# A graph attention kernel: the softmax's denominators are summed over partitions by VectorE instead of TensorE

## The chip, the core and the metric

The kernel runs on one core of a Trainium2 chip. A core has TensorE (PE: matrix products, and transposes by a product with the identity), VectorE (DVE), ScalarE (ACT), GpSimd (POOL) and SyncE (SP, which here only starts DMAs). Each works through a queue of its own in order, and semaphores tie the queues together. The metric is the device time of one execution in microseconds (us). SBUF is the on-chip memory of 128 partitions, PSUM the memory that TensorE writes; a quadrant is a group of 32 partitions.

## What is computed

x is 3327 x 512, adj is 3327 x 3327 with ones in about 1% of its places and zeros elsewhere. Two graph attention layers are followed by a layer norm, a binarized linear layer with an aggregation over adj, and another layer norm.

```python
def _gat_layer(x, W, adj):
    proj = x @ W
    Wh, Ws = jnp.split(proj, 2, axis=-1)
    scores = Wh @ Ws.T
    a = jax.nn.softmax(scores, axis=-1) * adj
    out = a @ Wh
    out = out + x
    return jax.nn.leaky_relu(out, NEG_SLOPE)
...
x = _layernorm(x + _L0_gnn_ref(x, adj, L0_gnn_W_stack), axis=-1)
x = _layernorm(x + _L1_gnn_ref(x, adj, L1_gnn_weight), axis=-1)
```

The softmax runs over all 3327 nodes before adj masks it. So each output row needs a denominator: the sum of its 3327 exponentials, masked or not. The kernel divides by it at the end, on the finished row of a @ Wh.

## The kernel before, in words

The nodes are cut into 26 tiles of 128 rows. Two tiles make a pair of 256, so there are NQ = 13 pairs. For each of the two attention layers, project() prepares the operands, and attention() goes through 13 x 13 steps (g, q): g is the pair of output rows, q the pair of nodes that is summed over. Scores are held transposed: the 256 output rows of g lie along the free axis, the nodes of q on the partitions. All products of 256 x 256 blocks are done as seven products instead of eight, so that sums of blocks are formed on VectorE and GpSimd, and results are put together from PSUM on VectorE and ScalarE.

A step of the loop at L976 writes out by hand, in the order of a number between 0 and 1 that each piece of work carries, what the queues get. For attention step v that is:

- TensorE: the score products of a later pair (L582, banks Z, X, Y in PSUM), and for step v itself the seven products with the values (L808).
- ScalarE: copies of the score products out of PSUM (L599, L634, L639), and the exponential of step v + 3 (L730). TensorE's next product into a bank waits for the copy out of it.
- VectorE: sums that put the scores together (L609, L624, L630), the running maximum (L652), the subtraction of the column maximum for step v + 3 (L727), the running sum of exponentials for step v + 2 (L738), the mask by adj (L743), and in half of the steps block sums of adj and a check of it (L763, L772).
- GpSimd: four block sums of the masked scores (L781 to L784), which wait for L743, and which TensorE's L808 needs.
- SyncE: the loads.

The running sum (L738) leaves for each g a tile total[g] of 128 partitions x 2 x 256: on each partition, the exponentials of its share of the nodes, for the 256 output rows of g. When the last step of g is done, take_out() (L818) puts the rows together from PSUM (L831 to L842), and finish(g) (L844) hands back a list of functions, one of which is called in each following step at 0.7 (L1005). GpSimd first adds the two halves of total[g] (L847). The first of the functions is norm():

```python
for i in range(2):
    nc.tensor.transpose(pz[:, i], sm[:, ts(i, P)], ident)
nc.vector.reduce_sum(rz, pz, axis=AX.X)
nc.vector.reciprocal(rz, rz)
```

Two transposes on TensorE (L856) bring the 256 rows onto the partitions of a PSUM tile pz, VectorE sums each over the free axis (L857) and takes the reciprocal (L858). The functions behind it, residual(i), scale the rows by rz (L872), apply the leaky relu (L875), add x in the last layer (L879), and store through GpSimd's DMA queue. In the last layer sign(i), turn(i) and linear(i) follow: layer norm statistics and signs on VectorE (L887, L888, L890), transposes of the signs (L896, copied by L898) and the binary product (L906).

There are 13 such normalizations in each of the two layers, 26 in all. The last one of layer 0 (g = 12) stands between attention and the next layer's project(): behind it on VectorE are the two residuals and then block sums of the new operands (L206 to L210), which TensorE's L403 needs. In the last layer VectorE also forms sums for the final aggregation during the last pair g = 12 (product_sums, L1076: L213 to L216), and the normalization of g = 12 stands at the end of attention, where TensorE is filled with aggregation products (L1100).

Of the kernel before, what the change touches and what calls it, by code (L numbers as in the profile page):

```python
# [9 lines left out]
F32 = mybir.dt.float32  # L10
# [6 lines left out]
AX = mybir.AxisListType  # L17
PSUM = bass.MemoryType.PSUM

P = 128  # L20
CT = 4
CW = CT * P
B = 32
HW = CW // 2
# [6 lines left out]
def kernel(  # L31
# [8 lines left out]
    nc = tc.nc  # L40
# [9 lines left out]
    def rows(t):  # L50
        return min(P, N - t * P)
# [7 lines left out]
    def half_tiles(g):  # L59

        return (2 * g, 2 * g + 1)
# [8 lines left out]
    small = ctx.enter_context(tc.tile_pool(name="small", bufs=4))  # L70
    ps_ch = ctx.enter_context(tc.tile_pool(name="ps_ch", bufs=3, space=PSUM))
    ps_acc = ctx.enter_context(tc.tile_pool(name="ps_acc", bufs=4, space=PSUM))
    ps_tr = ctx.enter_context(tc.tile_pool(name="ps_tr", bufs=1, space=PSUM))
# [7 lines left out]
    ident = keep.tile([P, P], F32, name="ident")  # L81
# [30 lines left out]
    def load_rows(eng, dst, src, r):  # L112

        cut = r - r % 16
        engines = eng if isinstance(eng, tuple) else (eng,)
        if cut:
            engines[0].dma_start(out=dst[:cut], in_=src[:cut])
        if cut < r:
            engines[-1].dma_start(out=dst[cut:r], in_=src[cut:r])
# [431 lines left out]
    def attention(l, att):  # L551
# [5 lines left out]
        sc, top, total, off, adj, acc, gs, xs, ch = ({} for _ in range(9))  # L557
# [286 lines left out]
        def finish(g):  # L844

            sm = total[g][:, 0]
            nc.gpsimd.tensor_tensor(sm, sm, total[g][:, 1], ALU.add)  # L847
            pz = ps_tr.tile([P, 2, P], F32, tag="tr", name=f"pz_{l}_{g}")
            rz = small.tile([P, 2], F32, tag="rz", name=f"rz_{l}_{g}")
            hs = out_.pop(g)  # L850
            mine = half_tiles(g)
            held = {}

            def norm():
                for i in range(2):
                    nc.tensor.transpose(pz[:, i], sm[:, ts(i, P)], ident)  # L856
                nc.vector.reduce_sum(rz, pz, axis=AX.X)  # L857
                nc.vector.reciprocal(rz, rz)  # L858

            def fetch(i):  # L860
                t = mine[i]
                span = slice(t * P, t * P + rows(t))
                for name, src in (("xres", x1_d), ("x0", x)) if last else (("xres", x),):
                    xr = ring.tile([P, D], F32, tag="xr", name=f"{name}_{l}_{t}")
                    load_rows(nc.sync, xr, src[span, :], rows(t))
                    held[i, name] = xr

            def residual(i):
                t, hh = mine[i], hs[i]
                r = rows(t)  # L870
                span = slice(t * P, t * P + r)
                nc.vector.scalar_tensor_tensor(  # L872
                    hh[:r], hh[:r], rz[:r, i : i + 1], held[i, "xres"][:r], ALU.mult, ALU.add
                )
                nc.vector.scalar_tensor_tensor(  # L875
                    hh[:r], hh[:r], NEG_SLOPE, hh[:r], ALU.mult, ALU.max
                )
                if last:
                    nc.vector.tensor_tensor(hh[:r], hh[:r], held[i, "x0"][:r], ALU.add)  # L879
                load_rows(nc.gpsimd, h_d[span, :] if last else x1_d[span, :], hh, r)  # L880

            def sign(i):

                t, hh = mine[i], hs[i]
                r = rows(t)
                st = small.tile([P, 6], F32, tag="bn", name=f"bn_{t}")
                nc.vector.bn_stats(st[:r], hh[:r])  # L887
                nc.vector.bn_aggr(mv[:r, t, :], st[:r])  # L888
                ba = held[i] = att.tile([P, D], BF16, tag="ba", bufs=1, name=f"ba_{t}")
                nc.vector.tensor_scalar(ba[:r], hh[:r], mv[:r, t, 0:1], None, ALU.is_gt)  # L890

            def turn(i):
                r = rows(mine[i])
                pt = ps_tr.tile([P, KD, P], BF16, tag="tr", name=f"pbt_{mine[i]}")
                for k in range(KD):
                    nc.tensor.transpose(pt[:, k, :r], held[i][:r, ts(k, P)], ident_h[:r, :r])  # L896
                held[i] = att.tile([P, KD, P], BF16, tag="baT", bufs=1, name=f"baT_{mine[i]}")
                nc.scalar.copy(held[i][:, :, :r], pt[:, :, :r])  # L898

            def linear(i):  # L900

                t = mine[i]
                r = rows(t)
                pw = ps_tr.tile([P, D], F32, tag="tr", name=f"pxw_{t}")
                for k in range(KD):
                    nc.tensor.matmul(  # L906
                        pw[:r], held[i][:, k, :r], bw[k], start=(k == 0), stop=(k == KD - 1)
                    )
                if g >= NQ - 2:
                    nc.scalar.copy(xw[t][:r], pw[:r])  # L910
                    return
                xh = att.tile([P, D], F16, tag="ba", bufs=1, name=f"xwh_{t}")
                nc.scalar.copy(xh[:r], pw[:r])
                load_rows(nc.gpsimd, xw_d[t], xh, r)

            fetch(0)
            if not last:
                return [norm, lambda: residual(0), lambda: fetch(1), lambda: None,
                        lambda: residual(1)]
            free = [] if g == NQ - 1 else [lambda: None]  # L920
            return [
                norm, lambda: residual(0), lambda: (sign(0), fetch(1)), *free,
                lambda: turn(0), lambda: linear(0), lambda: residual(1), lambda: sign(1), *free,
                lambda: turn(1), lambda: linear(1),
            ]
# [50 lines left out]
        for v in range(-LOOK - 4, len(steps)):  # L976
            u = v + LOOK
# [33 lines left out]
            if last and 0 <= v - first_products < EARLY:  # L1011
                p = v - first_products
# [3 lines left out]
            if v >= 0 and steps[v][1] == NQ - 1:  # L1016
                later += finish(steps[v][0])
# [309 lines left out]
```

## Time and profile before

| what | before |
|---|---|
| time, median of 3 runs | 2633.66 us (2631.25 to 2634.98) |
| the profiled execution | 2629.29 us, its span 2627.5 us |
| VectorE busy | 2089.6 us, 4279 instructions |
| TensorE busy | 2594.9 us, 12656 matmuls |
| ScalarE, GpSimd busy | 788.1 us, 1098.4 us |
| L856, transposes into pz | 52, median 273 ns |
| L857, the sum from PSUM | 26, median 412 ns |
| L858, the reciprocal | 26, median 165 ns |
| L847, GpSimd's sum of halves | 26, median 737 ns |

The profile is one execution. Its page gives the busy time of each engine, the same in 40 slices of the span (each digit is tenths of a slice), the chain of work that ended last, and groups of instructions: line, engine, operation, output<-input, shapes, count | busy time, mean ns of one | idle time of the engine just before, and what ended it. A list of waits names who waited for whom: us in total, times, longest. A timeline line has the start, the time taken, engine, line, operation, and in brackets the idle time before it and what ended that. Matmuls are pipelined and each lasts longer than it holds its engine, so the distance between starts tells what one costs; on VectorE, too, an instruction may start a little ahead of the end of the one before.

### The profile page before, as it was taken

Reading aid. Unit: us, or ns where it says so; the run is one execution under the profiler, and the core shown is the slowest. Engines: PE = TensorE matmul, PEld = TensorE weight load, DVE = VectorE, ACT = ScalarE, POOL = GpSimd, SP = SyncE. Lnnn points to the kernel's source line nnn. Section 1 sums busy time; section 2 is a strip of 40 time slices with the busy share of each in tenths; the row PEclk is TensorE's granted clock in tenths of the full one; section 3 lists DMA queues with packets and bytes.
Section 4 is the critical chain, followed back from the end, with each engine's and each line's share of the span. In section 5 each row is a group of like instructions: output and inputs, shape, how many; then the busy total and the mean of one; then the engine's idle time right before and its main releaser. Section 6 shows DMA issues by size and latency. Waiting matters only on the chain. (4 is left out here: it accounts for less than half of the span.)

```text
span 2627.5 us, 40294 instructions
## 1 busy us (share of the span) xinstructions
PE 2594.9 (99%) x12656; PEld 2249.1 (86%) x12656; DVE 2089.6 (80%) x4279; ACT 788.1 (30%) x1954; POOL 1098.4 (42%) x2025
## 2 busy tenths in 40 slices
PE   9999999999999999999999999999999999999998
PEld 6888888888888888887888888888888888888787
DVE  5864888889898886677875689888898888767976
ACT  2323332333333332222232333333333333222143
POOL 2640344444444444546552134444444444455510
PEclk9999999999999999999999999999999999999999
DMA  6855777787777776797865678777777777677775
GB/s 202 297 196 177 241 239 266 239 275 253 264 243 244 263 245 222 237 256 243 295 235 182 226 229 277 248 236 266 240 275 249 236 267 238 223 262 257 265 246 176
DMA packets 308055, 639.17 MB, mean 243 GB/s; under 512 B 34855, under 2 KB 175745, under 8 KB 306298
## 3 DMA queue, kind: packets, MB, share of 16 engines
q1 hardware_dynamic: 272140, 530.29, 61.9%
q0 software_dynamic: 35664, 106.18, 11.0%
q8 instruction: 104, 1.70, 0.3%
q14 instruction: 117, 0.96, 0.1%
q10 hardware_dynamic: 30, 0.03, 0.0%
HBM read 529.69 MB, written 106.67 MB: 242 GB/s over the span
## 5 line engine op out<-in xcount | busy, mean ns | idle before, releaser
L582 PE MATMUL pZ<-gs,xs 128*128 128x256 f32 x2496 | 636.0, 379 | 1.3 <-ACT u L599 1.3
L781 POOL TENSOR_TENSOR as<-s 128x128 f32<-128x128 f32 x338 | 162.4, 480 | 1048.1 <-DVE s L743 720.1
L582 PEld LDWEIGHTS pZ<-gs,xs 128*128 128x128 f32 x2496 | 473.5, 190 | 66.7 <-ACT u L599 2.4
L808 PE MATMUL acc<-ws,s 128*128 128x256 f32 x1352 | 402.2, 379 | 0.0
L808 PE MATMUL acc<-wh,s 128*128 128x256 f32 x1352 | 355.7, 379 | 0.6 <-DVE s L743 0.4
L808 PE MATMUL acc<-ws,as 128*128 128x256 f32 x1352 | 349.8, 380 | 3.9 <-POOL as L783 3.6
L730 ACT ACTIVATE s<-s 128x512 f32<-128x512 f32 x338 | 213.4, 631 | 362.8 <-DVE s L727 362.5
L582 PE MATMUL pY<-gs,xs 128*128 128x256 f32 x1248 | 320.8, 379 | 1.4 <-ACT p L599 1.4
L808 PEld LDWEIGHTS acc<-ws,as 128*128 128x128 f32 x1352 | 255.1, 190 | 44.6 <-POOL as L783 5.7
L808 PEld LDWEIGHTS acc<-wh,s 128*128 128x128 f32 x1352 | 256.6, 190 | 36.3 <-DVE s L743 1.5
L808 PEld LDWEIGHTS acc<-ws,s 128*128 128x128 f32 x1352 | 255.1, 190 | 33.9
L652 DVE TENSOR_TENSOR top<-top,s 128x512 f32<-128x512 f32 x312 | 223.7, 730 | 71.6 <-ACT s L639 51.8
L582 PEld LDWEIGHTS pY<-gs,xs 128*128 128x128 f32 x1248 | 236.6, 190 | 35.4 <-ACT p L599 3.3
L727 DVE TENSOR_TENSOR s<-s,off 128x512 f32<-128x512 f32 x338 | 247.1, 731 | 0.1
L743 DVE TENSOR_TENSOR s<-s,adj 128x512 f32<-128x512 f32 x338 | 237.5, 703 | 9.5 <-DMA adj<-in_adjT_dram 0.7
L738 DVE TENSOR_TENSOR total<-total,s 128x512 f32<-128x512 f32 x312 | 232.3, 745 | 0.0
L599 ACT COPY u<-pZ 128x256 f32<-128x256 f32 x312 | 115.8, 371 | 347.2 <-PE pZ L582 345.6
L783 POOL TENSOR_TENSOR as<-s 128x128 f32<-128x128 f32 x338 | 207.5, 614 | 26.5
L808 PE MATMUL acc<-wh,as 128*128 128x256 f32 x676 | 202.5, 381 | 0.0
L782 POOL TENSOR_TENSOR s<-s 128x128 f32<-128x128 f32 x338 | 184.9, 547 | 27.4
L784 POOL TENSOR_TENSOR as<-s,as 128x128 f32<-128x128 f32 x338 | 181.0, 535 | 26.5
L624 DVE TENSOR_TENSOR s<-p,u 128x256 f32<-128x256 f32 x156 | 66.7, 428 | 145.8 <-ACT u L599 144.8
(220 smaller groups left out, 3866.0 us busy)
## 6 DMA issues: line engine op xcount, KB each, us to landing
ws<-ws_d SPq DMA_DIRECT2D x338, 512.0 KB, 3.8
xs<-xs_d SPq DMA_DIRECT2D x182, 512.0 KB, 5.7
adj<-in_adjT_dram SPq DMA_DIRECT2D x324, 256.0 KB, 4.3
xs<-xs_d SPq DMA_DIRECT2D x156, 384.0 KB, 6.2
gs_d<-gsp POOLq DMA_DIRECT2D x88, 256.0 KB, 2.9
gs<-gs_d SPq DMA_DIRECT2D x12, 1792.0 KB, 10.4
adj_d<-ab POOLq DMA_DIRECT2D x169, 112.0 KB, 4.1
ahl<-adj_d SPq DMA_DIRECT2D x78, 224.0 KB, 4.9
```

The lines of the kernel that those rows point to most:

```text
L582: nc.tensor.matmul(ch[bank], xs[c, q, a][:, k], gs[c][:, b, k], start=(start and k == 0), stop=(k == 1), skip_group_check=True,)
L599: nc.scalar.copy(ch[name], ch[bank])
L652: nc.vector.tensor_tensor(top[i], top[i], t, ALU.max)
L727: nc.vector.tensor_tensor(s, s, off[g].to_broadcast([P, 2, HW]), ALU.subtract)
L730: nc.scalar.activation(sc[g, q], sc[g, q], AF.Exp)
L738: nc.vector.tensor_tensor(total[g], total[g], sc[g, q], ALU.add)
L743: nc.vector.tensor_tensor(s, s, adj[g, q], ALU.mult)
L781: nc.gpsimd.tensor_tensor(s3, a11, a21, ALU.subtract)
L782: nc.gpsimd.tensor_tensor(a21, a21, a22, ALU.add)
L783: nc.gpsimd.tensor_tensor(s2, a21, a11, ALU.subtract)
L784: nc.gpsimd.tensor_tensor(s4, a12, s2, ALU.subtract)
L808: nc.tensor.matmul(acc[g][i // 2][:, i % 2], a[i], b[i], start=(q == 0 and i % 2 == 0), stop=(q == NQ - 1), skip_group_check=True,)
```

## The change

norm() no longer uses TensorE. VectorE transposes the 128 x 256 tile in blocks of 32 x 32 into the second half of total[g], which is no longer needed. In each block the sums over its 32 nodes are then sums along the free axis: one reduce gives 8 numbers on each partition. Each quadrant of partitions then holds the sums over its own 32 of the 128 partitions, so four copies bring the quadrants beside each other on the first one, a second reduce adds the four, and four copies carry the results to the quadrants where the rows of rz lie. The reciprocal stays. The PSUM tile pz is gone; three small SBUF tiles are new.

```diff
-            pz = ps_tr.tile([P, 2, P], F32, tag="tr", name=f"pz_{l}_{g}")
             rz = small.tile([P, 2], F32, tag="rz", name=f"rz_{l}_{g}")
...
             def norm():
-                for i in range(2):
-                    nc.tensor.transpose(pz[:, i], sm[:, ts(i, P)], ident)
-                nc.vector.reduce_sum(rz, pz, axis=AX.X)
+                w = P // B
+                part = small.tile([P, HW // B], F32, tag="zq", bufs=1, name=f"zq_{l}_{g}")
+                quad = small.tile([P, w, HW // B], F32, tag="z4", bufs=1, name=f"z4_{l}_{g}")
+                whole = small.tile([P, 2, w], F32, tag="z", bufs=1, name=f"z_{l}_{g}")
+                turned = total[g][:, 1]
+                nc.vector.transpose(turned, sm)
+                nc.vector.reduce_sum(
+                    part, turned.rearrange("p (r u) -> p r u", u=B), axis=AX.X
+                )
+                for a in range(w):
+                    nc.vector.tensor_copy(quad[:B, a], part[ts(a, B)])
+                nc.vector.reduce_sum(
+                    whole[:B].rearrange("p i r -> p (i r)"),
+                    quad[:B].rearrange("p a r -> p r a"), axis=AX.X,
+                )
+                for a in range(w):
+                    nc.vector.tensor_copy(rz[ts(a, B)], whole[:B, :, a])
                 nc.vector.reciprocal(rz, rz)
```

B is 32, P is 128, HW is 256. ts(a, B) is the a-th group of B partitions.

## The prediction

> **What bounds the kernel now.** I read the page first: busy shares, the slices, the chain that ended last. Then the groups of the lines concerned, TensorE's waits, and the timeline around each of the 26 normalizations.
>
> ```profile
> PE 2594.9 (99%) x12656; PEld 2249.1 (86%) x12656; DVE 2089.6 (80%) x4279; ACT 788.1 (30%) x1954; POOL 1098.4 (42%) x2025
> ...
> PE   9999999999999999999999999999999999999998
> ...
> DVE  5864888889898886677875689888898888767976
> ```
>
> TensorE is busy in 99% of the span, in every slice, at full clock (PEclk is 9 throughout): whatever leaves its queue shortens the kernel, unless another engine is then late. VectorE has 20% idle on average, but 8 and 9 tenths in the attention slices, so its cover has to be looked at place by place. The chain of waits says the same: its largest shares are TensorE's products (L1100, L808), and everything else is 1% or less.
>
> TensorE's waits over the whole span are few; these are the ones that matter here:
>
> ```profile
> PE acc L808 <- POOL as L783: 3.6, 4, 1.2
> PE pZ_wh L403 <- DVE s L207: 2.5, 1, 2.5
> PE agg L1100 <- DVE wh L214: 1.8, 1, 1.8
> ...
> PE pZ L582 <- ACT u L599: 1.3, 2, 0.6
> ```
>
> Behind all four stands VectorE: GpSimd's L783 waits for L743, ScalarE's L599 stands in its queue behind the exponential L730, which waits for L727. So there are already places where VectorE, and not TensorE, sets the pace.
>
> What is removed, from the timeline of TensorE:
>
> ```profile
> 362.45 1.03 PE L582 MATMUL pZ<-gs,xs 128*128 128x256 f32 x4
> 363.32 0.38 PE L856 MATMUL pz<-ident,total 128*128 128x128 f32 x2
> 363.54 0.60 PE L808 MATMUL acc<-wh,as 128*128 128x256 f32 x2
> ```
>
> The starts count, since the durations overlap: the pair of transposes holds the queue from 363.32 to 363.54, 0.22 us.
>
> [...] L99, one element, 153 ns; L857, 256 elements, 415 ns[...]. [...] No row of before moves between quadrants. [...] Here L736, a copy, takes 411 to 683 ns[...].
>
> **The change, part by part.** The instruction order of both programs is the same on all engines but for the lines of norm(): nothing else moves, and no DMA.
>
> Removed from TensorE: 52 transposes, 26 x 0.22 = 5.7 us at most. With them goes the PSUM tile and VectorE's wait for it (4.9 us, six times), all at places with much spare, so it is worth nothing. GpSimd's sum L847 stays, and VectorE now waits for it; the transposes waited for it already and stood ahead of the reduce, so it is over in time in every case, and I cost that wait at nothing.
>
> Added to VectorE, prices from these rows (busy, mean ns):
>
> ```profile
> L340 DVE STREAM_TRANSPOSE xT<-xr 128x512 f32<-128x512 f32 x44 | 47.9, 1096 | 0.0
> ...
> L857 DVE TENSOR_REDUCE rz<-pz 128x2 f32<-128x256 f32 x26 | 10.8, 415 | 4.9 <-PE pz L856 4.9
> ...
> L262 DVE STREAM_TRANSPOSE wTs<-wl 128x128 f32<-128x128 f32 x32 | 7.0, 276 | 0.0
> ...
> L99 DVE TENSOR_SCALAR there<-there 128x1 f32<-128x1 f32 x1 | 0.2, 153 | 0.0
> ```
>
> - Block transpose 128x256: L262 is 0.27 us for 128 elements, 0.13 of it elements; 256 give 0.40. At L340's rate (its reads are strided) it would be 0.55. I take 0.40.
> - Reduce to 8 sums: 0.41, as L857.
> - Reduce of 32 elements: [...]0.19, between L99's 0.15 and L98's 0.28 for 127.
> - Eight tiny copies, in two sets of four. Each is 0.15 (L99). Independent small instructions start early in this trace: after the reciprocal (0.17) the next starts 0.08 later. If the copies do so, a set is 3 x 0.08 + 0.15 = 0.39. But each copy after the first starts in another quadrant; if they are held, a set is 4 x 0.15 = 0.60. I take held, and keep 0.39 as the other end.
> - Five handovers where an instruction waits for its forerunner: 0.035 each (reduce 364.80 + 0.41, reciprocal 365.24), 0.17.
>
> Sum 0.40 + 0.41 + 0.60 + 0.19 + 0.60 + 0.17 = 2.37; minus the old reduce with its handover, 0.45: VectorE's queue grows by d = 1.9 us per normalization (1.5 if nothing is held), 50 us in all. It needs 1.9 us of cover each time. Queued behind it: L652 and L727, hence ScalarE's exponential L730 and the PSUM copies behind that, hence TensorE's next product into those banks; and L743, hence GpSimd's sums and TensorE's L808.
>
> How much cover there is I read from the timeline: from each L858 on, along VectorE's queue and those it releases, counting as spare only what an instruction waited for something else, to the first TensorE instruction that would be late. An example with none (VectorE has no gap from 1832.0 on):
>
> ```profile
> 1840.86 0.68 DVE L727 TENSOR_TENSOR s<-s,off 128x512 f32<-128x512 f32 x1
> ...
> 1841.58 0.63 ACT L730 ACTIVATE s<-s 128x512 f32<-128x512 f32 x1 [4.85 <-DVE s L727]
> ...
> 1842.11 0.35 ACT L599 COPY u<-pZ 128x256 f32<-128x256 f32 x1
> ...
> 1842.52 0.73 PEld L582 LDWEIGHTS pZ<-gs,xs 128*128 128x128 f32 x4 [1.05 <-ACT u L599]
> 1842.52 1.13 PE L582 MATMUL pZ<-gs,xs 128*128 128x256 f32 x4 [0.65 <-ACT u L599]
> ```
>
> TensorE already stands 0.65 us for this chain; anything added to VectorE ahead of it is added to the time. The 26 fall into three groups (start of the reduce, us):
> - Much spare, 2.7 to 6.2 us: 365, 684, 1001, 1074, 1136, 1195, 2238, 2314, 2378. Nothing is lost, the pair is gained: 9 x -0.22 = -2.0.
> - Some, 1.0 to 1.6, in sum 14.4: 526, 607, 845, 926, 1583, 1666, 1749, 1911, 1994, 2077. TensorE is late by 1.9 minus spare: 10 x 1.9 - 14.4 = +4.6.
> - Little, 0 to 0.8, in sum 1.9: 447 (0.45), 766 (0.38), 1243 (0.10, the end of layer 0: L403 waits for L207), 1832 and 2160 (0), 2437 (0.18: TensorE waits for L743 and L783 until 2474), 2486 (0.80: L896 waits for ba, L890). 7 x 1.9 - 1.9 = +11.4.
>
> In the last two groups the removed pair gives nothing, since TensorE would only wait longer. Sum -2.0 + 4.6 + 11.4 = +14.0 us. The profiled execution has a span of 2627.5 and a time of 2629.3, so it would come to 2643.3. It lies 4.4 below the median of the runs, 2633.7; the difference is put on that median: 2647.7.
>
> **The rivals.** (1) The copies overlap, d = 1.5: -2.0, +0.4 (some of the ten still gain), 7 x 1.5 - 1.9 = +8.6: +7.0, 2640.7. For it: the early starts seen above. Against: no such start in the trace crosses quadrants.
> (2) The copies are shut out by GpSimd. In 11 of the 26 places GpSimd's sums run beside where the new instructions will stand; six of these have little or some spare (1243, 1583, 1666, 1911, 1994, 2437), with about two instructions of 0.8 us: up to 6 x 1.6 = 9.6, I take 7: +21, 2654.7. Against: copies of 8 and 2 elements may slip between.
> (3) Not slower: VectorE's readers have the spare after all, since 20% of it is idle. One mechanism, the cover of the 19 places of groups two and three; it decides where d is under about 0.9 us, or the spare is a microsecond more than I read. If only 1243, 2437 and 2486 lose, at d = 1.9 4.6 us, against 23 x 0.22 = 5.1 gained: -0.4, 2633.2. All hidden: -5.7, 2628.0. Against: the waits at 1842.5 and 2170, already open before.
>
> That the change does nothing is excluded: TensorE's order loses exactly the 26 pairs.
>
> **How the numbers follow.** Forecast (held, 1.7 to 2.1 us) 0.57, own range 2643 to 2652; rival 1 0.20; rival 2 0.13; rival 3 0.10. About 0.2% (5.3 us) is what can be told from no change. Rival 1 ends within it in a third of its cases, the forecast hardly; rival 3 lies within it or below: faster 0.04, same 0.14, slower 0.82. The range leaves out most of rival 3 and the far end of rival 2: 2638 to 2656.
>
> **What would show it.** The new copies' rows: mean near 150 ns and starts 0.15 apart (0.08: rival 1; several at 0.5 and more with GpSimd busy: rival 2). Normalization to next instruction 2.4 us on VectorE against 0.52. TensorE's waits: L582 <- ACT L599 from 1.3 us to about 12, L403 <- L207 from 2.5 to above 4, L808 <- L783 up by over 1. VectorE busy up by about 50 us, TensorE down by 52 instructions. If TensorE's waits stay near those of before, the reading of spare was wrong; if they grow although the rows are short, the prices were.

## The result, and the profile after

| | before | after |
|---|---|---|
| median of five runs | 2633.66 us (2629.16 to 2634.98) | 2661.10 us (2659.04 to 2666.74) |
| ratio | | 1.0114, interval 1.0103 to 1.0125 |
| the profiled execution, its span | 2629.29, 2627.5 us | 2666.74, 2664.9 us |

The changed kernel is slower by 27.4 us between the medians, where 14.0 was forecast; 2661.1 lies outside the range. (The two medians alone give a ratio of 1.0104, inside the interval.) The profiled execution of after is the slowest of its five, and its span is 37.4 us above that of before. The traces show where those 37.4 us go; they overstate the 27.4.

From the page of after, the busy shares:

```profile
PE 2602.0 (98%) x12604; PEld 2244.8 (84%) x12604; DVE 2145.1 (80%) x4539; ACT 782.3 (29%) x1954; POOL 1099.7 (41%) x2025
```

TensorE has 52 instructions fewer and VectorE is busy for 55.5 us more, as forecast (52 and about 50). The rows of the new instructions, in the groups by line (busy us, mean ns of one, idle time before):

```profile
L861 DVE STREAM_TRANSPOSE total<-total 128x256 f32<-128x256 f32 x26 | 11.3, 434 | 0.0
L862 DVE TENSOR_REDUCE zq<-total 128x8 f32<-128x256 f32 x26 | 10.9, 420 | 0.9
L866 DVE COPY z<-zq 32x8 f32<-32x8 f32 x104 | 23.0, 221 | 2.0
L867 DVE TENSOR_REDUCE z<-z 32x8 f32<-32x32 f32 x26 | 5.1, 195 | 0.9
L872 DVE COPY rz<-z 32x2 f32<-32x2 f32 x104 | 16.9, 163 | 2.0
```

The prices were nearly right: 0.43 for 0.40, 0.42 for 0.41, 0.195 for 0.19, copies of 0.158 in the middle for 0.15. (For 32 elements a straight line between L99 of before, one element in 153 ns, and L98, 127 in 279 ns, gives an estimate of 184 ns; L867 took 195. The 0.41 came from L857, which reads PSUM and took 415 ns; L862 reads SBUF and took 420.) One normalization on VectorE's timeline, first in before and then in after:

```profile
364.80 0.41 DVE L857 TENSOR_REDUCE rz<-pz 128x2 f32<-128x256 f32 x1
365.24 0.17 DVE L858 RECIPROCAL rz<-rz 128x2 f32<-128x2 f32 x1
365.32 0.67 DVE L652 TENSOR_TENSOR top<-top,s 128x512 f32<-128x512 f32 x1
```

```profile
365.18 0.43 DVE L861 STREAM_TRANSPOSE total<-total 128x256 f32<-128x256 f32 x1
365.64 0.42 DVE L862 TENSOR_REDUCE zq<-total 128x8 f32<-128x256 f32 x1
366.10 0.68 DVE L866 COPY z<-zq 32x8 f32<-32x8 f32 x4
366.81 0.19 DVE L867 TENSOR_REDUCE z<-z 32x8 f32<-32x32 f32 x1
367.04 0.68 DVE L872 COPY rz<-z 32x2 f32<-32x2 f32 x4
367.75 0.17 DVE L873 RECIPROCAL rz<-rz 128x2 f32<-128x2 f32 x1
367.83 0.67 DVE L652 TENSOR_TENSOR top<-top,s 128x512 f32<-128x512 f32 x1
```

A set of four copies takes 0.68 us, not 0.60, and the copies start 0.172 us apart: each starts 13 to 14 ns after the one before has ended. From the transpose to the next instruction, 367.83 - 365.18, are 2.65 us, against 365.32 - 364.80 = 0.52 in before. So VectorE's queue grows by d = 2.13 us, not 1.9, at thirteen of the 26 places, by 2.35 to 2.6 at the twelve where GpSimd's sums run beside it, and by 5.0 at the end of layer 0.

TensorE's waits in after (us in total, times, longest), in the order of the list, and below them one of before:

```profile
PE pZ L582 <- ACT u L599: 13.1, 10, 2.4
PE pY L582 <- ACT p L599: 9.1, 9, 2.3
PE acc L808 <- POOL as L783: 5.6, 6, 1.6
PE pZ_wh L403 <- DVE s L207: 5.0, 1, 5.0
...
PE pD L582 <- DMA xs<-xs_d: 2.4, 3, 1.1
PE pX L582 <- DVE s L630: 2.1, 6, 0.4
PE agg L1115 <- DVE wh L214: 1.8, 1, 1.8
```

```profile
PE pY L582 <- ACT p L599: 1.4, 4, 0.5
```

The first went from 1.3 to 13.1 us (forecast: about 12), the third from 3.6 to 5.6, the fourth from 2.5 to 5.0, all as named. The second, which went from 1.4 us to 9.1, was not named. It leads to a part of the loss that was missed. The place at 1832 in before looks like this in after's timeline:

```profile
1864.69 0.68 DVE L727 TENSOR_TENSOR s<-s,off 128x512 f32<-128x512 f32 x1
...
1865.41 0.63 ACT L730 ACTIVATE s<-s 128x512 f32<-128x512 f32 x1 [6.69 <-DVE s L727]
1865.95 0.36 ACT L599 COPY u<-pZ 128x256 f32<-128x256 f32 x1
...
1866.35 2.07 PE L582 MATMUL pZ<-gs,xs 128*128 128x256 f32 x4 [2.39 <-ACT u L599]
```

The chain is that of the prediction, and the wait that was 0.65 us is 2.39.

**Where the loss lies.** Leaving out the transposes of norm(), the n-th product of TensorE is the same in both traces. The difference between its two start times is its shift, and the growth of the shift shows what TensorE has lost in a stretch, here from 3 us ahead of one normalization (a place) to 3 us ahead of the next:

| group of places | forecast | forecast's rule with the measured d | after less before |
|---|---|---|---|
| much spare, 9 | -2.0 | -2.0 | +1.8 |
| some, 10 | +4.6 | +8.3 | +17.2 |
| little, 7 | +11.4 | +13.6 | +17.9 |
| sum | +14.0 | +19.9 | +36.9 |

The rest of the 37.4 us lies ahead of the first normalization (0.4) and behind TensorE's last product. At 1243, the end of layer 0, d is 5.0 us, so that the rule would put +4.9 there, but TensorE lost only 2.2; the third column has 2.2 there. The residuals behind that normalization took 1.44, 1.66, 1.75 and 0.69 us in before, beside GpSimd's block sums, and 0.75, 0.69, 0.74 and 0.69 in after, where those sums had run beside the new copies instead. The middle group lost twice what even the measured d explains.

**A first reading of the difference.** Adjacency blocks go into a ring, two tiles that are used in turn (tag adj_b), from which a store (L766, adj_d<-ab) takes them away. The store is issued by GpSimd, in its queue behind L784, which needs VectorE's L743. One such store behind the place at 1749, and the next instruction that writes its tile, first in before and then in after:

```profile
1771.66 0.55 POOL L766 DMA_DIRECT2D adj_d<-ab  x1
...
1775.86 0.29 DVE L763 TENSOR_TENSOR ab<-adj 128x128 fp8e4<-128x128 f32 x1 [0.19 <-DMA adj_d<-ab]
```

```profile
1792.21 0.55 POOL L766 DMA_DIRECT2D adj_d<-ab  x1
...
1800.72 0.29 DVE L763 TENSOR_TENSOR ab<-adj 128x128 fp8e4<-128x128 f32 x1 [4.50 <-DMA adj_d<-ab]
1800.77 0.40 ACT L749 CAST ab<-adj 128x256 fp8e4<-128x256 f32 x1 [5.16 <-DMA adj_d<-ab]
...
1801.76 0.37 ACT L599 COPY p<-pY 128x256 f32<-128x256 f32 x1
...
1802.18 0.48 PE L582 MATMUL pY<-gs,xs 128*128 128x256 f32 x1 [2.29 <-ACT p L599]
```

The store issued at 1792.21 frees its tile some 8.5 us later; in before that took 4.2. VectorE and ScalarE, each with an instruction that writes the next block at the head of its queue, stand until then; the PSUM copy L599 stands behind ScalarE's instruction, and TensorE behind that copy. Over the span VectorE's and ScalarE's waits for such stores grew, in before and then in after:

```profile
ACT ab L749 <- DMA adj_d<-ab: 28.1, 17, 4.8
DVE ab L763 <- DMA adj_d<-ab: 22.1, 15, 3.5
```

```profile
DVE ab L763 <- DMA adj_d<-ab: 38.8, 23, 4.5
ACT ab L749 <- DMA adj_d<-ab: 38.5, 17, 5.2
```

Measured against TensorE's own progress, 44 of the 169 stores were issued over 1 us later than in before, by up to 2.4 us. At six of the ten places of the middle group (607, 926, 1583, 1749, 1911, 2077) TensorE was late a second time in this way, 21 to 32 us behind the normalization: 0.7 to 2.6 us each, 8.4 in sum. Without these six losses the group lost 8.8 us, and the rule with the measured d gives 8.3. The six stores were issued 1.4 to 2.0 us later than in before, and they also took 1.0 to 4.3 us longer to land.

### The profile page after: what moved, and what is told of

Read it like the earlier page. It is cut to its first block, busy times and chain, and to the rows that moved or that the text cites. A ratio compares the mean times of both kernels' runs of the same rounds, so it can differ in the third digit from the quotient of the medians.

```text
span 2664.9 us, 40425 instructions
## 1 busy us (share of the span) xinstructions
PE 2602.0 (98%) x12604; PEld 2244.8 (84%) x12604; DVE 2145.1 (80%) x4539; ACT 782.3 (29%) x1954; POOL 1099.7 (41%) x2025
## 5 line engine op out<-in xcount | busy, mean ns | idle before, releaser
L582 PE MATMUL pZ<-gs,xs 128*128 128x256 f32 x2496 | 638.7, 380 | 13.3 <-ACT u L599 13.1
L808 PE MATMUL acc<-ws,s 128*128 128x256 f32 x1352 | 402.2, 379 | 0.0
L808 PE MATMUL acc<-wh,s 128*128 128x256 f32 x1352 | 357.4, 381 | 0.7 <-DVE s L743 0.6
L808 PE MATMUL acc<-ws,as 128*128 128x256 f32 x1352 | 350.1, 380 | 6.0 <-POOL as L783 5.6
L808 PEld LDWEIGHTS acc<-ws,as 128*128 128x128 f32 x1352 | 254.9, 190 | 47.7 <-POOL as L783 8.5
L808 PEld LDWEIGHTS acc<-wh,s 128*128 128x128 f32 x1352 | 257.7, 191 | 37.3 <-DVE s L743 2.1
L808 PEld LDWEIGHTS acc<-ws,s 128*128 128x128 f32 x1352 | 255.1, 190 | 33.9
L582 PEld LDWEIGHTS pY<-gs,xs 128*128 128x128 f32 x1248 | 236.8, 190 | 45.2 <-ACT p L599 13.1
L743 DVE TENSOR_TENSOR s<-s,adj 128x512 f32<-128x512 f32 x338 | 238.4, 705 | 10.2 <-DMA adj<-in_adjT_dram 1.5
L599 ACT COPY u<-pZ 128x256 f32<-128x256 f32 x312 | 115.5, 370 | 304.1 <-PE pZ L582 301.1
L808 PE MATMUL acc<-wh,as 128*128 128x256 f32 x676 | 202.4, 381 | 0.0
L784 POOL TENSOR_TENSOR as<-s,as 128x128 f32<-128x128 f32 x338 | 181.5, 537 | 26.5
```

The costliest lines, as they stand in the source:

```text
L582: nc.tensor.matmul(ch[bank], xs[c, q, a][:, k], gs[c][:, b, k], start=(start and k == 0), stop=(k == 1), skip_group_check=True,)
L599: nc.scalar.copy(ch[name], ch[bank])
L743: nc.vector.tensor_tensor(s, s, adj[g, q], ALU.mult)
L784: nc.gpsimd.tensor_tensor(s4, a12, s2, ALU.subtract)
L808: nc.tensor.matmul(acc[g][i // 2][:, i % 2], a[i], b[i], start=(q == 0 and i % 2 == 0), stop=(q == NQ - 1), skip_group_check=True,)
```

## The experiments

Three theories stood at the start. A is the forecast's own, with the measured d: only what exceeds the spare of a place is added. B says that VectorE's delay is multiplied, by the stores that are issued and land later, and by TensorE's clock after long stalls. C says that reading and transposing the tile costs in itself. Every experiment was run beside the kernel before on the same chip; the medians of before were 2629.8 to 2631.7 us there, and differences are taken from the one beside it. Each diff is against the kernel after or before, as named ahead of it. Where a sum or a copy is left out, the reciprocal is taken of ones, and the softmax is then not normalized.

### Transposes and row sums only

Against after; the second row sum and the last four copies, in the gap, are left out too.

```diff
-                for a in range(w):
-                    nc.vector.tensor_copy(quad[:B, a], part[ts(a, B)])
...
-                nc.vector.reciprocal(rz, rz)
+                nc.vector.reciprocal(rz, ones[:, 0:2])
```

> The changed kernel without its second reduce and its eight copies; the reciprocal is taken of ones, so the rows are not divided by their sums. VectorE's queue then grows by about 0.4 us per normalization (0.47 + 0.42 against 0.53 us to the next instruction). Theory A (time added is what exceeds the spare of each place, nothing else): three places with no spare lose 0.3 each, nearly all others gain the 0.22 of the removed pair: -3 us against before. Theory B (whatever VectorE loses is multiplied, by stores of adj blocks that are issued and land later, and by TensorE's clock): the same sign only if no chain starts, -3 to +2. Rival C (the transpose or reading SBUF instead of PSUM is itself what costs): above +8.

Measured: 2627.14 us, ratio 0.999 (0.9983 to 0.9996), -3.1 us. d is 0.35 us at most places of its trace. C, which expected more than +8, falls: transpose and row sum cost no more than their time on VectorE.

### All copies within one quadrant

Against after:

```diff
-                    nc.vector.tensor_copy(quad[:B, a], part[ts(a, B)])
+                    nc.vector.tensor_copy(quad[:B, a], part[:B])
...
-                    nc.vector.tensor_copy(rz[ts(a, B)], whole[:B, :, a])
-                nc.vector.reciprocal(rz, rz)
+                    nc.vector.tensor_copy(same[:B, a], whole[:B, :, a])
+                nc.vector.reciprocal(rz, ones[:, 0:2])
```

The same eight copies of the same sizes, but none starts in another quadrant than the one before.

> The changed kernel with all eight copies reading and writing in the first quadrant, same count and sizes; the sums are not moved between quadrants and the reciprocal is of ones, so the rows are not divided by their sums. If crossing quadrants is what holds the copies, they start about 0.08 us apart instead of 0.17, and the normalization takes about 2.0 us to the next instruction instead of 2.66: theory A +6 us against before, theory B up to +12. If the copies are spaced by their own length whatever the quadrant, all stays as in the changed kernel: +25 to +29 us.

Measured: 2645.41 us, ratio 1.0054 (1.004 to 1.0067), +15.2 us. From its timeline on VectorE:

```profile
363.85 0.38 DVE L867 COPY z<-zq 32x8 f32<-32x8 f32 x4
364.26 0.20 DVE L868 TENSOR_REDUCE z<-z 32x8 f32<-32x32 f32 x1
364.50 0.37 DVE L873 COPY zs<-z 32x2 f32<-32x2 f32 x4
```

A set takes 0.38 us instead of 0.68, the copies 0.073 apart instead of 0.172: rival 1's picture, with 0.08 in the prediction. So the step to another quadrant is what held them, and it is worth 0.6 of d. The reciprocal no longer waits either, so d is 1.40 us at most places, and up to 1.84 beside GpSimd's sums. With these values the rule of spare gives +9.0 if the 3.7 us of the end of layer 0 are taken, and +6.5 with the 1.1 that TensorE lost there, so A is too small here as well, by 6 to 9 us. Rival 1, which put this case at +7, would have missed it in the same way.

### No sums at all

Against before:

```diff
-                for i in range(2):
-                    nc.tensor.transpose(pz[:, i], sm[:, ts(i, P)], ident)
-                nc.vector.reduce_sum(rz, pz, axis=AX.X)
-                nc.vector.reciprocal(rz, rz)
+                nc.vector.reciprocal(rz, ones[:, 0:2])
```

> Before without the two transposes and the reduce, and with nothing in their place: the reciprocal is of ones, so the rows are not divided by their sums. It shows what the removal is worth if it costs VectorE nothing. Theory A: 26 x 0.22 = 5.7 us gained, and 0.45 instead of 0.22 at the handful of places where TensorE waits for VectorE: -7 us. Theory B: more, since relief is multiplied like load: -8 to -14. If TensorE's queue were not the bound in the middle: 0 to -2.

Measured: 2624.14 us, ratio 0.9976 (0.9967 to 0.9985), -6.1 us. It bounds what can be gained with everything else as in before: about 6 us (the interval reaches from 4 to 9), and 5.7 of that would be TensorE's own pair, 26 x 0.22.

### Both: after, with the two transposes left on TensorE

Against after:

```diff
             def norm():
...
+                for i in range(2):
+                    nc.tensor.transpose(pz[:, i], sm[:, ts(i, P)], ident)
```

> The changed kernel, and the two transposes per normalization back on TensorE, their result unused: the load on VectorE without the relief of TensorE. Theory A: the pair is worth its 0.22 us only at the nine places with much spare, so +2 us against the changed kernel, +29 against before. If the removed pair were worth its time everywhere: +33 against before. Theory B as A, within the scatter of the changed kernel.

Measured: 2663.96 us, ratio 1.0127 (1.0111 to 1.0142), +33.8 us. Its interval overlaps that of after (1.0103 to 1.0125), so this does not tell whether the pair is worth something in the places that lose. Its trace is a second view of the same load on VectorE: the middle group loses 12.4 us there, not 17.2. The second losses stand at the same six places and come to 4.5 us instead of 8.4, and the rest is 7.9. So the rule's part nearly repeats, and the stores' part differs between executions.

### Four buffers for the adjacency blocks, in before and in after

The same edit against each of the two; the scores' ring gives up one buffer for the room.

```diff
-    SBUFS = LOOK + 3
+    SBUFS = LOOK + 2
...
-                [P, 7, P], F8, tag="adj_b", bufs=2, name=f"ab_{l}_{g}_{q}"
+                [P, 7, P], F8, tag="adj_b", bufs=4, name=f"ab_{l}_{g}_{q}"
```

> The kernel before, with four buffers instead of two for the blocks of the adjacency matrix (tag adj_b), and one buffer less for the scores' ring to make room. It is the partner of the next run. Every theory: within 4 us of the kernel before (0 to -4, since before's VectorE stood 22.1 us and its ScalarE 28.1 us for the stores adj_d<-ab to land, nearly all of it covered; a loss only if the missing buffer of the scores' ring is felt).

> The changed kernel with the same four and one less buffers. Theory A (only VectorE's own 2.13 us per normalization less the spare, no store involved): as far above its partner as the changed kernel is above before, +28 us. Theory B (part of the loss is made by the stores of adjacency blocks, which are issued later behind GpSimd's wait for VectorE, and for whose landing VectorE and ScalarE then stand): the waits for adj_d<-ab nearly vanish from VectorE and ScalarE, and it is no more than +20 us above its partner, as the rule of spare time with the measured 2.13 us gives (19.9).

Measured: before with it 2626.07 us, ratio 0.9979 (0.997 to 0.9988); after with it 2645.16 us, ratio 1.0056 (1.0042 to 1.007). The two lie 19.1 us apart, where B expected no more than 20, A 28. TensorE's waits in after with four buffers:

```profile
PE pZ L582 <- ACT u L599: 9.0, 8, 2.4
PE acc L808 <- POOL as L783: 5.3, 6, 1.3
PE pZ_wh L403 <- DVE s L207: 5.0, 1, 5.0
```

TensorE's wait for ACT p L599 (9.1 us in after) is gone from the list, and so are VectorE's and ScalarE's waits for adj_d<-ab. The largest that stay are those that the prediction named. At each of the six places the second loss is 0.0 us beside the partner.

### The normalization by a column of ones

Against before:

```diff
-                    nc.tensor.transpose(pz[:, i], sm[:, ts(i, P)], ident)
-                nc.vector.reduce_sum(rz, pz, axis=AX.X)
-                nc.vector.reciprocal(rz, rz)
+                    nc.tensor.matmul(
+                        pz[:, i : i + 1], sm[:, ts(i, P)], ones[:, 0:1], start=True, stop=True
+                    )
+                nc.vector.reciprocal(rz, pz)
```

> The kernel before, with the two transposes and VectorE's row sum replaced by two matmuls against a column of ones, so that TensorE sums over partitions and VectorE only takes the reciprocals, from PSUM. VectorE's queue loses the row sum of 0.45 us in each normalization. Both theories: between the kernel without sums (-6.3 us) and before: -3 us, -1 to -6. If the matmuls with one column cost TensorE as much as the transposes, it is above -1.

Measured: 2632.37 us, ratio 1.0008 (1.0002 to 1.0015), +2.6 us. A gain of about 3 us was expected, so this is a miss. Its timeline on TensorE:

```profile
361.98 1.03 PE L582 MATMUL pZ<-gs,xs 128*128 128x256 f32 x4
362.84 0.50 PE L856 MATMUL pz<-ones,total 128*128 128x1 f32 x4
363.20 0.68 PE L808 MATMUL acc<-wh,as 128*128 128x256 f32 x2
363.72 0.59 PE L808 MATMUL acc<-ws,s 128*128 128x256 f32 x2
```

Two products with one column are four instructions here (x4), and they hold the queue for 0.36 us, where the two transposes held it for 0.22; the next two take 0.52 instead of 0.43. That is 0.23 us more per normalization, 26 x 0.23 = 6 us at most. In its trace the first two groups lose 4.9 us, the first place left out, and the third gains 2.2 by VectorE's shorter queue: +2.7 in sum. At the first place its trace loses 4.5 us more; VectorE waits there 5.3 us for a store adj_d<-ab.

### The same work in two portions

Against after; norm() ends behind the first four copies, and rest() runs one step later.

```diff
                 for a in range(w):
                     nc.vector.tensor_copy(quad[:B, a], part[ts(a, B)])
+                held["quad"] = quad
+
+            def rest():
...
                 nc.vector.reduce_sum(
                     whole[:B].rearrange("p i r -> p (i r)"),
...
-                return [norm, lambda: residual(0), lambda: fetch(1), lambda: None,
+                return [norm, lambda: (rest(), residual(0)), lambda: fetch(1), lambda: None,
...
-                norm, lambda: residual(0), lambda: (sign(0), fetch(1)), *free,
+                norm, lambda: (rest(), residual(0)), lambda: (sign(0), fetch(1)), *free,
```

> The changed kernel, with the same instructions in two portions: transpose, row sums and the first four copies where the normalization stood, the second row sum, four copies and the reciprocals one tile step later, ahead of the first residual. Each portion adds 1.0 to 1.1 us where the whole added 2.13. Theory A: two portions find spare time twice, +6 to +12 us above before. Theory B, where each delay is multiplied by stores issued later: +15 to +20. If VectorE's total work counted and not the length of one block: +28, as the changed kernel.

Measured: 2661.88 us, ratio 1.0122 (1.0106 to 1.0137), +32.1 us, as after. My expectation from A, that spare time is found twice, was wrong. Before's windows suggest the reason (length, then the busy us of PE, PEld, DVE, ACT and POOL with the number of instructions in brackets, granted clock, share of DMA, GB/s):

```profile
364.80:378.50 13.70, 13.70 (x65) 12.05 (x65) 13.32 (x30) 4.49 (x12) 5.54 (x11) 1.00 0.77 240
1831.00:1845.00 14.00, 13.36 (x63) 11.43 (x61) 13.55 (x29) 3.54 (x10) 5.78 (x12) 1.00 0.75 270
```

Third among the busy times is VectorE: 13.3 of 13.7 us after the first normalization, 13.6 of 14.0 at the place without spare. VectorE has next to no gap for two steps, so it makes up nothing between the portions, and the reader behind both meets the same 2.1 us. As I read it, the spare of a place is the lead that ScalarE and TensorE have over VectorE's results, not a gap in VectorE. The trace fits in the middle group: without the second losses it loses 7.5 us, near the 8.8 and 7.9 of the two unsplit traces. The second losses are smaller, 3.6 us, but the split lost that elsewhere: at the two places without spare TensorE stood 3.2 us each instead of 2.4, and it ran 20.5 us at half clock where after had 10.2 (both without the tail of the kernel). Why those stalls grew was not followed.

### VectorE's sums only where nothing was lost

Against before:

```diff
+            free_here = 8 <= g < (NQ - 2 if last else NQ - 1)
...
+                if free_here:
...
+                else:
+                    for i in range(2):
+                        nc.tensor.transpose(pz[:, i], sm[:, ts(i, P)], ident)
+                    nc.vector.reduce_sum(rz, pz, axis=AX.X)
```

Ahead of the else stand the changed kernel's sums.

> VectorE's sums in the seven normalizations alone at which the changed kernel's TensorE lost nothing but gained the two transposes (row pairs 8 to 11 of the first layer, 8 to 10 of the second); TensorE's transposes as before in the other nineteen. If the cost belongs to the place, by what is free there: 7 x -0.22 = -1.5 us against before (-3 to 0). If each normalization costs its share of the whole: 7/26 of +28 = +7.5 us.

> The same with four buffers for the adjacency blocks and one less in the scores' ring. If the two edits act on different waits, they add up: -5.5 (the four buffers in before) and -1.5, together -7 us against before. If the four buffers already made room at those places, no more than -5.5.

Measured: 2629.43 us, ratio 0.9992 (0.9984 to 1.0001), -1.4 us against a shared +7.5; and with four buffers 2624.45 us, ratio 0.9974 (0.9964 to 0.9984), -6.4 us. The cost does belong to the place. A gain of 1.5 us is below what these runs can tell from nothing. (One of the seven places, 1136, had lost 1.9 us in after's trace, in a wait for the DMA of xs; the other six had gained.)

### The store from SP's queue, in after and in before

The same edit against each of the two:

```diff
-            nc.gpsimd.dma_start(out=adj_d[g][:, q], in_=adj.pop((g, q, "b")))
+            nc.sync.dma_start(out=adj_d[g][:, q], in_=adj.pop((g, q, "b")))
```

> The changed kernel, with the adjacency blocks' store issued from SP's queue in place of GpSimd's, two buffers as in before. If the store's late issue behind GpSimd's wait for VectorE makes the extra loss: the waits for adj_d<-ab shrink by half or more and the time comes near that with four buffers, +15 to +20 above before. If the transfer's own landing (3.9 us in the middle) or the two buffers make it, whoever issues: +26 to +30, as the changed kernel. If SP's queue is itself held by loads that wait for buffers: above +30.

> The partner of the run with the store on SP's queue: the kernel before with the adjacency blocks' store issued from SP. If the store's late issue made the extra loss of the change, this kernel gains less from the move than the changed one did (16 us): -2 to -6 against before, as with four buffers (-4.5), which leaves +16 to +20 for the change beside it, the rule of spare time with the measured 2.13 us (19.9). If the move simply makes any version faster, it gains the same 13 to 16 us, and the change still costs its +28.

Measured: after with it 2644.09 us, ratio 1.0051 (1.0037 to 1.0065); before with it 2623.02 us, ratio 0.9966 (0.9954 to 0.9978). From VectorE's waits in after with the store on SP:

```profile
DVE ab L763 <- DMA adj_d<-ab: 7.4, 4, 3.2
```

It was 38.8 us, and the second loss at the six places is again 0.0 us beside the partner. In TensorE's progress, SP issues the store 4.6 us earlier (the middle one of 169) than GpSimd did in before, although it then takes longer to land (5.4 us in the middle instead of 3.9). So with two buffers and a slower transfer the stores leave the path once their issue does not stand behind GpSimd's wait for VectorE. This does not divide the loss between the later issue and the longer landing of after's six stores, since an issue 4.6 us earlier covers both. Before gained 8.7 us by the move, more than the 2 to 6 expected, and after 14 to 17 (from its +27.4 between medians, or +30 by the ratio). With the stores out of the way the change costs 21.9 us (13.2 above and 8.7 below the before beside each). Before with the store on SP is the fastest full kernel here. Most of its 8.7 us is not explained: its profiled execution is only 3.7 us shorter than before's, and the move also takes the issues themselves, 169 of 0.56 us, out of GpSimd's queue; no run separates the two.

## Why the prediction missed

**The removed pair and the order.** This part was right: 52 transposes went, and six of the nine places of the first group gained 0.22 us each in the traces, no more. (365 and 684 lost 0.7 and 0.5 us, and 1136 lost 1.9 us in a wait for the DMA of xs.) Without any sums the kernel gains 6.1 us, the forecast's 5.7 within the noise.

**The term d** was of the right kind and too small. The copies were held, as the prediction took it, but they stand 0.172 us apart instead of 0.15, and the handovers are longer. d is 2.13 us (2.35 to 2.6 beside GpSimd) instead of 1.9, which moves the rule's sum from 14.0 to 19.9 us. That is 5.9 of the 13.4 us that the forecast is short between the medians. That a change of quadrant would hold the copies was an assumption of the forecast, which nothing in before showed; the later traces do: the copies start 0.172 us apart in after, across quadrants, and 0.073 in the run with all eight in one.

**The step that failed is the path:** the cover was read "along VectorE's queue and those it releases", only "to the first TensorE instruction that would be late", and the delay of the stores was put at nothing ("nothing else moves, and no DMA"). For the first instructions the reading nearly held: without its second losses the middle group lost 8.8 us, and the rule gives 8.3. But GpSimd's queue carries the delay on. L784 waits for VectorE, the store is issued behind it, and the next block waits for the store's tile. In before VectorE stood 0 to 0.8 us for a store at the six places; in after those stores landed 2.6 to 5.8 us later in TensorE's progress, and TensorE was late a second time. The shift of TensorE's products shows it by group:

| group | rule with the measured d | after less before | four buffers, after less before | store on SP, after less before |
|---|---|---|---|---|
| much | -2.0 | +1.8 | -4.7 | -2.4 |
| some | +8.3 | +17.2 | +7.3 | +7.4 |
| little | +13.6 | +17.9 | +14.7 | +12.8 |
| sum | +19.9 | +36.9 | +17.3 | +17.8 |

With the stores off the path, in either way, the middle group loses 7.3 and 7.4 us, near the rule's 8.3; with them on it, 17.2 in this trace and 12.4 in that of both. (The -4.7 holds one wait of before with four buffers for xs, 1.9 us at 1156, which its partner does not have.) In the timed runs the change costs 19.1 and 21.9 us beside the two partners, and 27.4 without: so about 5 to 8 us of the median run are the stores', and the rest is near the rule with d as measured. (The rule's 19.9 has the 2.2 us seen at the end of layer 0; with its own 4.9 there it gives 22.6.) By the ratios the change costs 1.0077 and 1.0085 in place of 1.0114; each of the two has an uncertainty of about 0.0017, so the share of the stores is known to within some 5 us only, and it is the traces that show the mechanism.

**What the sum had no term for** is TensorE's clock. Around the ends of the two 2.39 us stalls of the third group the granted clock falls to 0.5 for 3.41 us. These are the windows of after around the stall at 2203 (the column behind the five engines is the granted clock):

```profile
2200.60:2204.00 3.40, 1.01 (x5) 0.64 (x4) 3.37 (x7) 1.16 (x3) 0.74 (x2) 1.00 0.78 218
2204.10:2207.50 3.40, 3.40 (x10) 2.72 (x9) 3.33 (x7) 1.36 (x4) 2.10 (x5) 0.51 0.77 292
2207.60:2211.00 3.40, 3.40 (x18) 2.99 (x17) 3.26 (x9) 0.41 (x2) 1.98 (x5) 1.00 0.00 0
```

TensorE does ten products against 18 in the same time: 3.4 us at half clock cost some 1.7. Two such stretches, 3.2 us by the shift, are in the profiled execution of after and of both its partners with the stores out of the way, and in none of before's at those places; they are in the third row of the table. They are not certain: the trace of both has stalls of 2.38 and 2.37 us at these places and no low clock. Nor is TensorE at full clock throughout in before, as the prediction reads from its slices of 66 us: behind the wait for L207, at 1250, before has 3.41 us at half clock too.

**The chain** on which the prediction also leans covers only 6% of the span (TensorE 5%, L808 rounds to 0%), so it says nothing of the attention steps. The forecast's sum does not rest on it.

**The rivals.** Rival 1's early starts came in the run with all copies in one quadrant (0.073 us apart); the changed copies do not stay in one, and start 0.172 apart. Rival 2's delay beside GpSimd is there and small: d grows by 0.2 to 0.5 us at twelve places, among them five of the six that the rival had named at up to 1.6 us each. The first set's copies have a mean of 221 ns against 158 in the middle, and only at the sixth, the end of layer 0, is a copy held up to 1239 ns. In before L736, a copy too, took 411 to 420 ns in the 14 places where GpSimd's instructions ran beside it for less than 0.1 us, and 673 to 683 in the 12 where they did so for 0.39 to 0.73. That GpSimd shuts a copy out is not shown by that: no run tests that it is GpSimd that holds them. Rival 2 came nearest in time, for the wrong reason. Rival 3 needed a microsecond more spare than I read, and the reading was about right for the first reader. (It speaks of 19 places in groups two and three; they have 17.)

**What stays open:** why the six stores take longer to land than in before, and why a single one lands 8.5 us after issue when the middle one takes 3.9. No run took the crowd of loads around them apart.

## What to carry to other kernels

When an engine is to be slowed, do not stop at the first reader that would be late. Follow also the DMAs that are issued behind instructions waiting for that engine, and what stands until they land; a wait for such a DMA is no cover where the DMA comes later too, as six stores did here, by 2.6 to 5.8 us. Where VectorE had no gaps (13.3 us busy of 13.7), delay was not made up between steps, and splitting the added work gained nothing (ratio 1.0122 against 1.0114). And try to issue a store that frees a small ring from a queue that does not wait for the engine refilling the ring: here that move was worth 8.7 us to the kernel before.

## What was not expected of the hardware

- TensorE's granted clock fell to 0.5, mostly for 3.41 us, around stalls of 2.0 us and more, though not at each. Between the kernels' start and end all 14 traces together have 22 stalls of 1.96 to 2.63 us, of which 16 had a low clock and six had none; all eight stalls of 3.1 us and more had one, and none of the eight from 1.54 to 1.93 us, nor had the wait for L214, 1.83 us in before and 1.84 in after. In after the clock was at 0.5 for 3.41 us around each of the stalls of 2.39, 2.39 and 4.98 us, and not at that of 2.29; in before around that of 2.46.
- A float32 product with a single column held TensorE for 0.18 us in the run with the column of ones, longer than a 128 x 128 transpose in before with its 0.11.
- A tiny copy on VectorE cost 0.172 us in after, where it starts in another quadrant than the one before, and 0.073 in the run with all copies in one quadrant, for 8 and for 2 elements alike.
